# Turning the second attention step's queries and keys on TensorE, and an earlier memset, in a four-layer float32 kernel on one core

## The chip, the core and the metric

One of the eight cores of a Trainium2 chip runs the whole program. Its engines are TensorE (PE in the profile; PEld is its weight load), VectorE (DVE), ScalarE (ACT), GpSimd (POOL) and SyncE (SP, which here only issues DMAs). Each has its own queue, worked off in order, and they wait for each other by semaphores. The metric is the device time of one execution in microseconds (us), lower is better; a time is the median of several runs. One further execution is recorded by the profiler; all rows shown are of that one.

## What is computed

The reference takes `x` of (8, 128, 512), float32, and adds four layers to it one after the other. Cut to what matters here:

```python
x = x + _L0_ffn_ref(_L0_cond_ref(x, ...), ...)
x = x + _L1_ffn_ref(_L1_cond_ref(x, ...), ...)
x = x + _L2_ffn_ref(_L2_cond_ref(x, ...), ...)   # attention, then an expert mix
x = x + _L3_ffn_ref(_L3_cond_ref(x, ...), ...)
```

Layer 2 begins with attention over 32 query heads and 8 key heads of 128 numbers, with a paged cache of 512 keys and values per sequence and 128 new ones:

```python
q = _rope(_rmsnorm(q, q_norm_w), pos)
k = _rope(_rmsnorm(k, k_norm_w), pos)
k_all = jnp.concatenate([kc, k], axis=1)
scores = jnp.einsum('bqhd,bkhd->bhqk', q, k_all) * SCALE
probs = jax.nn.softmax(jnp.where(valid, scores, -1e+30), axis=-1)
o = jnp.einsum('bhqk,bkhd->bqhd', probs, v_all)
```

The result `o` goes through `Wo` and becomes the input of the expert mix.

## The kernel before, in words

The four layers run one after the other, with the work of one beginning among the last work of the layer ahead of it. Layer 2's attention is cut into 32 steps (`steps`): 8 key heads times 4 pairs of sequences. A step `n` handles one key head, its four query heads (`REP`) and two sequences (`j` = 0, 1). Its parts are:

- `project` (products `q_one`, `q_six`, `q_five`, line 971): queries, keys and values of the new tokens, by a scheme of seven block products for eight. It uses PSUM tiles of the tags `mm` (three of them) and `st` (three). The copies and adds that empty them are at lines 1020 and 1025.
- `squares`, `roots`, `rotate`, `rotated`, `normed`: the norm and the rotary turn. GpSimd makes the crossed terms `vq` and `vk` (line 1070). In the first two steps it also makes the inverse root (`roots`, lines 1093 and 1094, by a power). VectorE multiplies by it at line 1104. The result is the tile `r` with ten blocks of 128x128, eight of queries and two of keys.
- Turning: the scores need queries and keys with the head's dimension on the partitions. From step 1 on this takes three moves. `turn(n)` lets VectorE transpose 32x32 blocks into `qkt` (line 1127) and writes it to DRAM in four DMAs (`written`, line 1120). `fetch(n)` reads it back in another order with three DMAs, into `qT` (line 1153) and `kTn` (line 1155); both tiles have one buffer. Step 0 is turned otherwise, by `turn_at_once(0)`: ten transposes on TensorE (line 1145, `turned`) into PSUM, and three copies by ScalarE (line 1147).
- Cached keys and values: `gather(n, "k")` and `gather(n, "v")` issue eight indirect DMAs each from GpSimd's queue (line 914, `kn` and `vals`). `turn_cached` transposes the keys in blocks on VectorE (line 1111, `kt`), and they go through DRAM into `kT` in the same way.
- `weigh(n, j)`: the scores (`st`, line 1165, ten products a sequence) and their exponentials on ScalarE (`pT`, line 1169).
- `mix(n, j)`: products of the weights with the values (`av`, line 1217, ten a sequence), into tiles of the tag `av`, of which there are two.
- `added`, `summed`, `inverted`, `divided`: the sums of the weights, the inverse through DRAM into `R` (line 1210), and the division (`oT`, line 1227).
- `leave(n - 1)`: the output product with `Wo` (`wo_one`, `wo_two`, `wo_six`, line 971), added up in `y2` over the key heads. `y2` is therefore set to zero first, by a memset of 128x4096 numbers on GpSimd (line 1319).

Two functions set the order. `first` makes steps 0 and 1's projections between the last products of layer 1 (`eo_l`, `midp_l`, `midTp_l`, lines 53 and 283, with routing work on VectorE at lines 244 to 272). `run` then goes through the steps; while step `n`'s weights are made, step `n + 1` is projected and turned and step `n - 1` leaves. For `n` = 0 nothing is projected or leaves, since step 1 was projected in `first`.

What is wrapped in `kept` stays in the order in which it is written, on each engine, once `running` holds something; on GpSimd it always does. What isn't wrapped is placed by a scheduler: the memset of `y2` was written at the head of `run`, but it was put behind the gathers of step 1's keys, ahead of step 0's `vq`.

Of the kernel before, what the change touches and what calls it, by code (L numbers as in the profile page):

```python
# [17 lines left out]
P = 128  # L18
NB = 8
# [773 lines left out]
def attention(tc, a, x, ident, lens, kvrow, part, ww, wop, ypool, sums, rot, eps, psa, c2, chunks, mm):  # L793
# [66 lines left out]
    def kept(i):  # L860
        return tc.keep_in_program_order(i) if running or i.ins.engine == pool.engine else i
# [38 lines left out]
    def every(ops):  # L900
        for _ in ops:
            pass
# [186 lines left out]
    def roots(n):  # L1089
        s = S[n]  # L1090
        s["rs"] = rs = wk.tile([P, 2, REP + 1], F32, tag="rs", name=f"rs_{n}")
        if n < 2:
            kept(pool.tensor_scalar(rs, s["ssq"], 1.0 / HD, EPS_RMS, ALU.mult, ALU.add))
            kept(pool.tensor_tensor(rs, rs, half, ALU.pow))
        else:
            kept(act.activation(rs, s["ssq"], AF.Sqrt, bias=eps, scale=1.0 / HD))
# [25 lines left out]
    def turn(n, by=(sp,)):  # L1122

        s = S[n]
        m = 2 * REP
        t = wk.tile([P, 4, m + 2, 32], F32, tag="kt", name=f"qkt_{n}", bufs=1)
        done = kept(dve.transpose(t, s["both"].rearrange("p m (b d) -> p b m d", b=4)))
        s["qT"] = wk.tile([P, 4, m, 32], F32, tag="qT", name=f"qT_{n}", bufs=1)
        s["kn"] = wk.tile([P, 2, 4, 32], F32, tag="kTn", name=f"kTn_{n}", bufs=1)
        written(turned_new[n], t, by)  # L1130
        return done

    def turn_at_once(n):

        s = S[n]
        m = 2 * REP
        s["qT"] = qT = wk.tile([P, 4, m, 32], F32, tag="qT", name=f"qT_{n}", bufs=1)
        s["kn"] = kn = wk.tile([P, 2, 4, 32], F32, tag="kTn", name=f"kTn_{n}", bufs=1)
        for h in (slice(0, REP), slice(REP, m), slice(m, m + 2)):
            k = h.stop - h.start  # L1140
            ps = psa.tile([P, k, P], F32, name=f"turned_{n}_{h.start}", **(
                dict(tag="av") if k == REP else dict(tag="st", bufs=3)
            ))
            for i in range(k):
                kept(pe.transpose(ps[:, i, :], s["both"][:, h.start + i, :], ident))
            to = qT[:, :, h, :].rearrange("p a m t -> p m a t") if k == REP else kn
            kept(act.copy(to, ps.rearrange("p m (a t) -> p m a t", t=32)))

    def fetch(n):
        s = S[n]  # L1150
        m = 2 * REP
        src = turned_new[n].rearrange("b i a m d -> (b i) a m d")
        kept(sp.dma_start(s["qT"], src[:, :, 0:m, :]))
        for j in range(2):
            kept(sp.dma_start(s["kn"][:, j], src[:, :, m + j, :]))
# [32 lines left out]
    def summed(n, j):  # L1188


        s = S[n]
        if j == 0:
            s["rows"] = wk.tile([P, 4, 2, REP * 4], F32, tag="rows", name=f"rows_{n}", bufs=1)
        t = wk.tile([P, REP * 4, 32], F32, tag="part10", name=f"partT_{n}_{j}", bufs=1)
        kept(dve.transpose(t, s["part", j].rearrange("p (b d) -> p b d", d=32)))
        kept(dve.tensor_reduce(s["rows"][:, 0, j, :], t, AX.X, ALU.add))  # L1196
# [91 lines left out]
    def first(mixed, outs_):  # L1288

        every(tokens(0))  # L1290
        running.append(True)
        later = tokens(1, "pT")
        project(0, {
            "u2": lambda: turn_cached(1)(),
            "c22": lambda: every(later),
            "c11": lambda: (squares(0, "k", 0, (0,)), squares(0, "q", 0, (0, 1))),
            "c12": lambda: squares(0, "q", 0, (2, 3)),
        })
        keys_terms = rotate(0)
        mixed()  # L1300

        def rest():
            squares(0, "q", 1, range(REP))
            squares(0, "k", 1, (0,))
            roots(0)
            keys_terms()
            outs_(0)
            outs_(1)
            rotated(0)
            normed(0)  # L1310
            outs_(2, 3)

        project(1, {"one": rest, "c11": lambda: turn_at_once(0)})

    def run(pool_, end_of, bank, keep):
        late.append(pool_)
        y2 = ypool.tile([P, NB, D], F32, tag="y", name="y2")
        Y.append(y2)
        pool.memset(y2, 0.0)

        squares(1, "q", 0, range(REP))
        keys_terms = rotate(1)
        squared(1)
        keys_terms()
        roots(1)
        gather(1, "v")
        rotated(1)
        normed(1)
        turn(1)
        end, prepared = None, iter(())  # L1330
        w_ops, wo_ops = iter(()), WO[0].factors()

        def some(ops, k=1):
            return lambda: [next(ops, None) for _ in range(k)]

        for n, (qd, p) in enumerate(steps):

            after = n + 1 if 0 < n < len(steps) - 1 else None
            weigh(n, 0)
            sums_of, outs = added(n, 0), iter(())  # L1340
            if n == 1:
                some(wo_ops, 2)()
            next(sums_of)
            (some(wo_ops) if n == 1 else some(w_ops))()
            every(sums_of)
            every(w_ops)
            if n:
                divided(n - 1)
                outs = outputs(n - 1)
                if not after:  # L1350
                    every(outs)
            if after:
                project(after, {
                    "u2": lambda: every(outs),
                    "c22": lambda: (turn_cached(2)() if n == 1 else None, some(wo_ops, 3)()),
                    "c11": lambda: (squares(after, "k", 0, (0,)), squares(after, "q", 0, (0, 1))),
                    "c12": lambda: squares(after, "q", 0, (2, 3)),
                })
                keys_terms = rotate(after)
                if n + 2 < len(steps):  # L1360
                    if steps[n + 2][1] == 0:
                        weights(steps[n + 2][0])
                    gather(n + 2, "k")
                leave(n - 1, {
                    "one": lambda: (
                        squares(after, "q", 1, range(REP)), squares(after, "k", 1, (0,)), roots(after),
                    ),
                    "c22": lambda: (every(wo_ops), keys_terms(), rotated(after), normed(after), turn(after)),
                })
                fetch(after)  # L1370
                gather(after, "v")
            mixed = mix(n, 0)
            left = (lambda: leave(n - 1),) if n and not after else ()
            weigh(n, 1, {2: (some(mixed), *left), 3: (some(mixed),), 4: (some(mixed, NC),)})
            sums_of = added(n, 1)
            next(sums_of)
            summed(n, 0)
            if n == 0:
                next(sums_of)
                fetch(1)  # L1380
                gather(2, "k")
            every(sums_of)
            summed(n, 1)
            if 0 < n < len(steps) - 2 and steps[n + 2][1] == 0:
                w_ops = W[steps[n + 2][0]].factors()
            inverted(n, some(w_ops))
            if n + 2 == len(steps):
                end.load_w2()
                end.load_aw()
            if left:  # L1390
                end.shifted()
            if n == 0:
                every(tokens(2))
            if n == 5:
                prepared = end.prepare(bank, lambda shape, name: wk.tile(shape, F32, tag="xs", name=name, bufs=1))
            next(prepared, None)
            every(mix(n, 1))
            next(prepared, None)
            if n and p == 0:
                out_weights(qd)  # L1400
                wo_ops = WO[qd].factors()
            if 0 < n < len(steps) - 2:
                turn_cached(n + 2)()
                some(w_ops)()
                every(tokens(n + 2))
            if n == 3:
                kept(keep())
            if n == 4:
                end = end_of(kept)

            if qd == NQ - 1 and p:
                for j in range(2):
                    end.turn(y2, 2 * (p - 1) + j, bank)
            if n + 2 == len(steps):
                end.low(0, bank)
                end.anchors(0, bank)
        divided(n)
        every(outputs(n))
        end.product(0, "st", bank)
        leave(n)  # L1420
        return y2, end
# [903 lines left out]
```

## Time and profile before

| | us |
|---|---|
| median of 5 runs | 1503.55 |
| lowest and highest | 1501.98 and 1507.11 |
| the profiled execution | 1508.1 |
| its span, from the first to the last instruction | 1506.2 |
| TensorE busy | 1483.0 (98%) |
| VectorE busy | 1070.5 (71%) |
| GpSimd busy | 854.2 (57%) |
| ScalarE busy | 561.3 (37%) |
| mean granted TensorE clock | 0.996 of full speed |

How to read rows of it: in the chain of waits a row is the start, the duration, the engine and the line (`L1165` is line 1165 of the kernel before); the chain is followed back from the last instruction, so what stands in it set the end. In the timeline a row is start, duration, engine, line, operation, output and inputs, the number of instructions run together, and in brackets the idle time ahead of it with what ended it. In the list of waits a row is who waited for whom, the time in total, how often, and the longest. In the tables by stretch a row gives, for PE, PEld, DVE, ACT and POOL, the busy time, and then the granted TensorE clock, the DMA share and GB/s. All times count from the span's start.

### The profile page before, as it was taken

Reading aid. Unit: us, or ns where it says so; the run is one execution under the profiler, and the core shown is the slowest. Engines: PE = TensorE matmul, PEld = TensorE weight load, DVE = VectorE, ACT = ScalarE, POOL = GpSimd, SP = SyncE. Lnnn points to the kernel's source line nnn. Section 1 sums busy time; section 2 is a strip of 40 time slices with the busy share of each in tenths; the row PEclk is TensorE's granted clock in tenths of the full one; section 3 lists DMA queues with packets and bytes.
Section 4 is the critical chain, followed back from the end, with each engine's and each line's share of the span. In section 5 each row is a group of like instructions: output and inputs, shape, how many; then the busy total and the mean of one; then the engine's idle time right before and its main releaser. Section 6 shows DMA issues by size and latency. Waiting matters only on the chain.

```text
span 1506.2 us, 18126 instructions
## 1 busy us (share of the span) xinstructions
PE 1483.0 (98%) x5619; PEld 942.4 (63%) x5619; DVE 1070.5 (71%) x2122; ACT 561.3 (37%) x1419; POOL 854.2 (57%) x874
## 2 busy tenths in 40 slices
PE   8999999999999999999999999999999999999997
PEld 7888787455555565555555555565555555569886
DVE  4566524378788887877778777778877878854475
ACT  1111101044444555444455445455445455431110
POOL 2232103647777677777677777677777777622210
PEclk9999999999999999999999999999999999999999
DMA  7311001204546444454443455445445534432001
GB/s 238 117 43 32 1 1 53 95 29 129 172 136 200 124 145 120 150 175 134 136 153 117 129 155 182 124 134 152 130 128 165 167 105 136 116 123 79 2 15 44
DMA packets 157145, 172.74 MB, mean 115 GB/s; under 512 B 53616, under 2 KB 127536, under 8 KB 156912
## 3 DMA queue, kind: packets, MB, share of 16 engines
q1 hardware_dynamic: 138896, 134.48, 30.2%
q0 software_dynamic: 17056, 36.49, 7.7%
q8 instruction: 47, 0.77, 0.2%
q10 hardware_dynamic: 1088, 0.52, 0.1%
q14 instruction: 58, 0.48, 0.1%
HBM read 130.01 MB, written 41.42 MB: 114 GB/s over the span
## 4 chain that ended last, share of the span: by engine, by line
PE 88%; DVE 5%; DMA 4%; issue 1%; ACT 0%; SPq 0%; ACTq 0%; DVEq 0%
PE st L1165 17%; PE av L1217 15%; PE g L362 8%; PE q_six L971 8%; PE q_one L971 5%; PE q_five L971 5%; PE wo_two L971 5%; PE dn L362 5%; PE wo_one L971 3%; PE wo_six L971 3%; PE eo_l L53 3%; DMA qT<-turned_new 2%; PE h L1753 2%; PE z L1753 2%; PE midp_l L53 1%; PE o L1753 1%
## 5 line engine op out<-in xcount | busy, mean ns | idle before, releaser
L914 POOL DMA_INDIRECT kn<-in_k_cache,kvrow_k x256 | 270.9, 1058 | 76.7 <-issue 66.0
L914 POOL DMA_INDIRECT vals<-in_v_cache,kvrow_v x256 | 270.9, 1058 | 73.5 <-issue 48.2
L1217 PE MATMUL av<-pT,vals 128*128 128x512 f32 x640 | 290.6, 592 | 0.2 <-DVE oT L1227 0.2
L1169 ACT ACTIVATE pT<-st,hide 128x512 f32<-128x512 f32 x256 | 176.0, 687 | 196.4 <-PE st L1165 196.3
L1165 PE MATMUL st<-qT,kT 128*128 128x512 f32 x512 | 238.3, 598 | 4.8 <-DMA qT<-turned_new 4.6
L1217 PEld LDWEIGHTS av<-pT,vals 128*128 128x128 f32 x640 | 121.4, 190 | 153.1 <-issue 145.9
L1070 POOL TENSOR_TENSOR vq<-q,txq 128x256 f32<-128x256 f32 x128 | 121.2, 978 | 144.0 <-ACT sqq L1044 100.8
L1165 PEld LDWEIGHTS st<-qT,kT 128*128 128x128 f32 x512 | 96.6, 191 | 116.6 <-issue 101.7
L1185 DVE TENSOR_TENSOR part<-pT 128x512 f32<-128x512 f32 x128 | 88.4, 692 | 81.3 <-ACT pT L1169 77.0
L971 PE MATMUL q_one<-q,x 128*128 128x384 f32 x256 | 93.0, 486 | 0.0
L1044 ACT ACTIVATE sqq<-q 128x128 f32<-128x128 f32 x252 | 78.2, 310 | 10.7 <-DVE q L1020 4.1
L971 PEld LDWEIGHTS q_one<-q,x 128*128 128x128 f32 x256 | 48.5, 190 | 39.8 <-issue 14.4
L971 PE MATMUL q_six<-q_s,xs_all 128*128 128x384 f32 x192 | 69.8, 486 | 0.0
L1025 ACT COPY q<-q_one 128x256 f32<-128x256 f32 x32 | 11.9, 372 | 148.9 <-PE q_one L971 142.8
L971 PE MATMUL wo_one<-o,oT 128*128 128x256 f32 x256 | 65.8, 379 | 0.4 <-DVE oT L1227 0.4
L1165 PE MATMUL st<-qT,kTn 128*128 128x512 f32 x128 | 65.4, 592 | 0.0
L971 PE MATMUL wo_two<-o_s,os 128*128 128x256 f32 x256 | 60.5, 379 | 0.3 <-DVE os L930 0.3
L429 POOL TENSOR_TENSOR ws<-wu 128x256 f32<-128x256 f32 (+1 forms) x9 | 6.4, 713 | 92.0 <-DMA wu<-in_WuT 81.7
L1169 ACT ACTIVATE pT<-st,rs 128x512 f32<-128x512 f32 x64 | 44.0, 687 | 38.5 <-PE st L1165 38.5
L971 PEld LDWEIGHTS wo_one<-o,oT 128*128 128x128 f32 x256 | 48.6, 190 | 13.9 <-DVE oT L1227 0.6
L1201 ACT COPY rows<-rows 32x32 f32<-32x32 f32 x96 | 20.7, 216 | 97.3 <-DVE rows L1196 96.5
L362 PE MATMUL g<-xs,ws 128*128 128x256 f32 (+1 forms) x240 | 56.1, 384 | 0.0
(459 smaller groups left out, 2850.8 us busy)
## 6 DMA issues: line engine op xcount, KB each, us to landing
turned_new<-qkt SPq DMA_DIRECT2D x124, 160.0 KB
turned_cached<-kt SPq DMA_DIRECT2D x128, 128.0 KB
kT<-turned_cached SPq DMA_DIRECT2D x32, 512.0 KB
R<-sums SPq DMA_DIRECT2D x32, 512.0 KB
qT<-turned_new SPq DMA_DIRECT2D x31, 512.0 KB
q<-in_WqT SPq DMA_DIRECT2D x8, 1024.0 KB
o<-in_WoT SPq DMA_DIRECT2D x8, 1024.0 KB
kn<-in_k_cache,kvrow_k POOLq DMA_INDIRECT x256, 2.8
```

The source lines that it names most:

```text
L53: pe.matmul(o, lhsT, rhs, start=start, stop=stop)
L362: pe.matmul(o, lhsT, rhs, start=start, stop=stop, skip_group_check=True)
L914: kept(pool.indirect_dma_start(out=d[:, c, :], out_offset=None, in_=kc if what == "k" else vc, in_offset=bass.IndirectOffsetOnAxis(ap=kvro ...
L971: kept(pe.matmul(o, l[:, c, :], r[:, c, :], start=start and c == 0, stop=c == 1, skip_group_check=True))
L1044: kept(act.activation(sq, S[n][m][:, j, i, :], AF.Square, accum_out=S[n]["ssq"][:, j, col : col + 1]))
L1070: kept(pool.tensor_tensor(to, t[:, b, :, hi : hi + 64], wx[:, b, lo : lo + 64].unsqueeze(2).to_broadcast(list(to.shape)), ALU.mult,))
L1165: kept(pe.matmul(ps, s["kT"][:, c, 4 * j : 4 * j + 4, :] if c < 4 else s["kn"][:, j], s["qT"][:, :, REP * j : REP * (j + 1), :].rearrange( ...
L1169: kept(act.activation(pT[:, c, :, :].rearrange("p i t -> p (i t)"), ps, AF.Exp, **(dict(bias=hide[:, b, c : c + 1]) if c < 4 else dict(bia ...
L1185: kept(dve.tensor_tensor(o, l, r, ALU.add))
L1201: kept(act.copy(rows[0:32, g, :], rows[32 * g : 32 * g + 32, 0, :]))
L1217: kept(pe.matmul(ps, v[:, c, :], pT[:, c, :, :].rearrange("p i t -> p (i t)"), start=c == 0, stop=c == NC - 1, skip_group_check=True,))
L1753: return pe.matmul(o, lhsT, rhs, start=start, stop=stop, skip_group_check=True)
```

## The change

It has two parts.

The memset of `y2` moves from the head of `run` into `first`, directly behind `roots(0)`, so behind step 0's power on GpSimd. It is wrapped in `kept`: its place on GpSimd is then as written.

Step 1's queries and keys are turned by `turn_at_once(1)` and no longer by `turn(1)` and `fetch(1)`. VectorE's block transpose, four writes and three reads of that step go away; ten TensorE transposes and three ScalarE copies come in. They are written behind the adds of step 0's second sequence, so on TensorE they stand behind the products of step 0's first sequence with the values and ahead of those of the second. Both `av` tiles are in use there, so all three PSUM tiles of step 1's turning are of the tag `st`; step 0 keeps `av` for two of its three. Steps 2 to 31 are turned as before.

```diff
@@ turn_at_once
             ps = psa.tile([P, k, P], F32, name=f"turned_{n}_{h.start}", **(
-                dict(tag="av") if k == REP else dict(tag="st", bufs=3)
+                dict(tag="av") if n == 0 and k == REP else dict(tag="st", bufs=3)
             ))
@@ first, rest
             roots(0)
+            y2 = ypool.tile([P, NB, D], F32, tag="y", name="y2")
+            Y.append(y2)
+            kept(pool.memset(y2, 0.0))
             keys_terms()
@@ run
         late.append(pool_)
-        y2 = ypool.tile([P, NB, D], F32, tag="y", name="y2")
-        Y.append(y2)
-        pool.memset(y2, 0.0)
-
+        y2 = Y[0]
         squares(1, "q", 0, range(REP))
...
         normed(1)
-        turn(1)
         end, prepared = None, iter(())
...
             if n == 0:
                 next(sums_of)
-                fetch(1)
                 gather(2, "k")
             every(sums_of)
+            if n == 0:
+                turn_at_once(1)
             summed(n, 1)
```

## The prediction, made before the change was run

> **What bounds the kernel now.** The page comes first. TensorE (PE) is busy for 1483.0 of 1506.2 us, so what counts is where its stream breaks. The list of what TensorE waited for has two waits of more than 2.1 us:
>
> ```profile
> PE 1483.0 (98%) x5619; PEld 942.4 (63%) x5619; DVE 1070.5 (71%) x2122; ACT 561.3 (37%) x1419; POOL 854.2 (57%) x874
> ...
> PE st L1165 <- DMA qT<-turned_new: 4.6, 5, 2.8
> PE midTp_l L283 <- DVE mw_l L272: 2.9, 1, 2.9
> ```
>
> The second number is the count, the last the longest one. Both are places that the diff touches. The chain of waits around them, and the rows of the timeline, follow.
>
> ```profile
> 292.98 3.76 DVE s_l L268
> ...
> 298.04 0.95 PE midTp_l L283 x4
> 298.99 0.91 PE midp_l L53 x4
> 299.89 4.45 PE eo_l L53 x8
> ...
> 293.17 3.53 POOL L1319 MEMSET y<- 128x4096 f32 x1
> L268 DVE TENSOR_SCALAR s_l<-s_l x6: 160/170/3750, 233.7 to 1438.6; 128x4 f32<-128x4 f32 x6
> L820 DVE TENSOR_SCALAR hide<-hide x1: 1178/1178/1178, 250.7 to 250.7; 128x32 f32<-128x32 f32 x1
> 250.62 2.48 POOL L830 TENSOR_TENSOR txk<-wx_k,sin 128x512 f32<-128x512 f32 x2
> ```
>
> A `tensor_scalar` on four numbers per partition takes 0.17 us (the median of six) and once 3.75. That one ended at 296.73, when the memset of `y2` on GpSimd (POOL) ended, 296.70. The same is seen at 250.7: `hide` ended at 251.88, together with the first of the two POOL products that began at 250.62. So this form of VectorE (DVE) instruction stands still while POOL runs. TensorE paid: its last product before had ended at 295.13 and it went on at 298.04.
>
> ```profile
> 338.35 5.13 PE av L1217 x12
> 343.48 4.46 DMA qT<-turned_new
> 347.93 0.04 issue
> 347.98 6.26 PE st L1165 x10
> ...
> 298.00:299.00 1.00, 0.96 (x5) 0.99 (x6) 0.49 (x1) 0.00 (x0) 0.00 (x0) 0.60 0.00 0
> 300.00:301.00 1.00, 1.00 (x2) 0.48 (x3) 0.00 (x0) 0.37 (x1) 0.00 (x0) 0.50 0.00 0
> 350.00:351.00 1.00, 1.00 (x2) 0.34 (x1) 1.00 (x3) 0.57 (x1) 0.69 (x2) 0.50 0.12 33
> 415.11 4.29 PE st L1165 x10
> ```
>
> Here TensorE ends its `av` products at 345.22 and starts step 1's scores at 347.98, when the turned queries came back from DRAM. In the window rows the third number from the end is the granted clock: 0.50 after either idle time. Step 1's ten score products take 6.26 us, against 4.29 in step 3 (415.11). So each of the two waits costs twice: once itself, once the dip.
>
> **Part 1, the memset leaves 293.17.** Without it, L268 ends at about 293.15; L269, L270 and L272 (0.18, 0.19, 0.69 us and the gaps between) end at 294.3, before TensorE has its last `t` product behind it (eight at 0.43 from 291.43: 294.87). So the transposes start at 294.87, and at full clock take 0.44 (the four at 314.05 do) and not 0.95. The next, `midp_l`, needs `l` (L304, 0.68 us behind the end of `t` at 295.13), so it starts near 295.9 and takes 0.46. The eight `eo_l` take 3.43 (as at 315.78) and end near 299.8. Before, 304.34: 4.5 us. The short hold-up before `midp_l` may cost what one of 0.42 us did at 382.60 (4.56 for 4.29), so I take 4.3. Bounds: 2.91 + 1.98 (0.51 + 0.45 + 1.02 of dip) = 4.9 above; nothing below, if L268 does not meet the memset in most executions. L268 started only 0.19 us before the memset, so a POOL that ran half a microsecond later would let it through. Behind this the stretch to 345 is one TensorE stream with waits of at most 0.2 us, and its other inputs are early: `kn` of step 1 is issued by 293.17 and read at 309.40, and `kT` of step 0 is fetched from 290.20 and used at 327.88. So the gain stays.
>
> **Part 2, the memset arrives behind the power.** On POOL the first power ends at 321.56 and the next work, `vq` of step 1, starts at 327.37 after 5.81 us of idle time that a VectorE result ended. The memset (3.53) fits with 2.28 to spare: POOL's later work, the gathers among it, is not put off. What VectorE does in 321.56 to 325.09 is `r<-r,rs` (L1104), two `x<-eo_l,x` (L300) and two `uq` (L984, L986), all TENSOR_TENSOR. Price: 0 if these ignore POOL, at most 3.53 plus a dip of 1.98 = 5.5 if L1104, which TensorE's `turned` waits for, stands still as L268 did. The nearest row: L1075, `r<-q,tsq` 128x1024, took 1.24 us at 314.65 in the middle of POOL's `vq` products (313.39 to 317.34), and 1.23 and 1.26 at 328.63 and 396.77. I take 0. The Trainium skill (SBUF — State Buffer, Who interferes with whom) says that a VectorE instruction with two SBUF inputs is blocked by a GpSimd one that reads SBUF, not by one that only writes. By it L1075 should have stood still beside `vq`, which the row does not show; for a memset, rule and row both give 0, and the sum is the same by either.
>
> **Part 3, step 1 turned by TensorE.** Removed: VectorE's transpose L1127 (1.51 at 337.32), four writes and three reads on SP's queue (L1120, L1153, L1155; 1.76, 0.61 and 1.29 us of issue), and the wait 2.76 with its dip 1.97. Added, behind step 0's first `av` (six products left from 338.35: 340.93) and ahead of its second: ten transposes, 1.09 us as at 324.37, and three ACT copies, 0.61, 0.61, 0.41. ACT is idle from 339.08 to 347.29, and the bank of each `st` tile is free at 339.08, so the copies are done by 343. The input `r` is ready at 337.29, 3.6 early. The ten `av` left run from 342.0 to 346.3, and step 1's scores follow at once, at full clock, to 350.6 instead of 354.23: 3.64 earlier (2.76 + 1.97 - 1.09). What stood behind the removed issues comes earlier too: VectorE's row sums by 1.5, so `R` is fetched at 349.3 and not 350.83, lands some 3.9 later (the last `R` took 3.92), and `oT` (L1227), its reader, cannot start before 353.5, since the adds ahead of it fill VectorE: no wait.
>
> **Part 4, what is late next.** POOL does not get those 3.64 us. Its 16 gathers follow the second power back to back:
>
> ```profile
> 336.20 2.03 POOL L914 DMA_INDIRECT vals<-in_v_cache,kvrow_v  x1 [0.18 <-issue]
> ...
> 357.48 0.95 POOL L914 DMA_INDIRECT kn<-in_k_cache,kvrow_k  x1 [0.30 <-issue]
> ...
> 360.61 1.29 DVE L1111 STREAM_TRANSPOSE kt<-kn 128x512 f32<-128x512 f32 x2
> 361.83 0.65 DVE L878 TENSOR_TENSOR o_s<-o,o_s 128x512 f32<-128x512 f32 x1
> 362.40 0.41 DVE L1020 TENSOR_TENSOR q<-q_five,uq 128x256 f32<-128x256 f32 x1
> ```
>
> (Part 1 moves all times here alike; I leave it out.) A gather of `kn` lands 2.8 us after its issue (median of the DMA list), so the last, 357.48, lands at 360.3, at the latest by 361.26, when the second `kt` transposed it without a wait. VectorE, 2.6 us earlier by then, wants it at 358.65 and stands for 1.6 to 2.6 us. Behind it in VectorE's queue is `q<-q_five` (L1020), whose PSUM bank the product `wo_two` takes: it becomes free at 362.2 to 363.0 instead of 363.0, while TensorE, 3.6 early, has ended `wo_one` at 360.33. TensorE so stands for 1.9 to 2.7 us and starts `wo_two` 0.8 to 1.7 earlier than before. An idle time of 2.03 us, at 25.12, was followed by a dip: sixteen `g` products took 5.24 from 28.23, and 3.56 from 56.63 (1.7 more). With that the scores of step 2 are reached at 382.2 give or take 0.5, against 382.18; and their own turned queries hang on the same `q`, so they land 0 to 0.85 before 382.56. Net of parts 3 and 4: 0.3 gained of 3.64; between 0.7 lost and, if the gathers land early enough, all 3.64. The skill's page on this (TensorE: Matmul & The Clock Gate, Part 1) wants about 3.4 us without work for a dip; the rows here show one after 2.03, 2.76 and 2.91. By the page TensorE would reach step 2's scores between 380.5 and 381.4 and wait for the fetch, 0 to 0.85 gained, and the whole sum would be near 4.7.
>
> **The sum.** 4.3 + 0 + 0.3 = 4.6 us. The profiled execution took 1508.1 us, 1.9 more than its span, so it becomes 1503.5. It lies 4.55 above the median of the five runs, 1503.55; the same gain there gives 1499.0.
>
> **Rivals.**
> *The gathers land in time*, and part 3 keeps its 3.64: 4.3 + 3.6 = 7.9, 1495.7. For it: no wait is seen at 360.61. Against it: a 2.8 us landing leaves at most 1.0 us of room where 2.6 would be needed.
> *The profiled execution is not the usual one*: it is slower than the median by 4.55 us, nearly the 4.3 of part 1. If L268 slips by the memset in most timed runs, only 0.3 is left: 1503.2. Against it: POOL and VectorE both run down from one product (the end of `t`, 281.7), with little to set them apart, and any memset that starts up to 3.5 us earlier blocks L268 also.
> *The memset stops VectorE at its new place*: L1104 begins at 321.60, 0.04 us behind the power, just as the memset does. If it stands still until 325.09, `turned` comes 2.0 us late, the queue behind it 3.5, and the dip adds 1.98: 5.5 lost against 4.6 won, 1504.5. It decides from 4.6 us on. Against it is the row of L1075.
>
> **How the numbers follow.** Chances: my sum 0.48, gathers in time 0.15, no usual meeting 0.22, memset in the way 0.10, something else 0.05. A difference of 0.2% (3.0 us) is about what a measurement can tell here. Faster by that: most of the first (its gain lies between 3 and 5), the second, a little of the third: 0.60. Within: the rest of the third, half of the fourth and odd ends: 0.28. Slower: half of the fourth, whose price has no row from above, and the unknown: 0.12. The range reaches from the first rival to the third, 1495.5 to 1504.5. My sum's own range is 1497.5 to 1501.
>
> **What would show it.** Part 1: L268 at 0.17 us every time, no wait of `midTp_l`, clock 1.00 through 295 to 300. Part 2: the memset directly behind the power, L1104 at 1.23. Part 3: no wait for `qT` before step 1, scores in 4.29. Part 4: a wait of `kt` for `kn` of 1.6 to 2.6 us, and `wo_two` held by `q`; if `kt` doesn't wait, the first rival is right. I am wrong on the first term if the changed kernel's median is within 2 us of 1503.55 while its profile shows L268 short.

## The result

| | before | after |
|---|---|---|
| median, us | 1503.44 (56 runs) | 1497.06 (29 runs) |
| lowest and highest | 1498.10 and 1509.87 | 1492.78 and 1501.81 |
| profiled execution | 1508.1 | 1497.81 |
| its span | 1506.2 | 1496.0 |

The ratio is 0.9962, 95% interval 0.9953 to 0.9970: the change saves 5.7 us of 1503.44, and the interval reaches from 4.5 to 7.1. The medians lie 6.4 apart, the two profiled executions 10.3.

The page of the changed kernel has TensorE at work for all but 16.1 us of the span; before it was all but 23.2:

```profile
PE 1479.9 (99%) x5629; PEld 942.0 (63%) x5629; DVE 1065.9 (71%) x2121; ACT 562.3 (38%) x1422; POOL 855.6 (57%) x874
```

Its list of what TensorE waited for (total, times, longest) no longer has `midTp_l`, nor any wait of `st` for `qT`. The longest one left, of `gu`, was there before (2.0); the one of `wo_two` is new:

```profile
PE gu L362 <- DVE tgm L369: 2.0, 1, 2.0
PE wo_two L971 <- DVE vals L1020: 1.4, 1, 1.4
```

**Around the old place of the memset.** The rows of L268 in the changed kernel, and then its chain of waits (start, duration, what):

```profile
L268 DVE TENSOR_SCALAR s_l<-s_l x6: 158/170/171, 233.9 to 1430.2; 128x4 f32<-128x4 f32 x6
```

```profile
291.68 3.71 PE t L53 x8
...
295.41 0.70 DVE l L304
...
296.16 0.73 PE midp_l L53 x4
296.89 3.43 PE eo_l L53 x8
```

L268 takes 0.17 us every time, the longest of the six being 171 ns. The eight `eo_l` end at 300.32 and take 3.43, no dip: before, they took 4.45 and ended at 304.34. `t` begins 0.25 later here, so the gain is 4.27 at this point. From the start of `t` to step 0's first scores it was 36.45 us (291.43 to 327.88) and is 32.19 (291.68 to 323.87): 4.26 less.

**Around the memset's new place, and step 1's turning.** The timeline of the changed kernel:

```profile
317.51 3.51 POOL L1308 MEMSET y<- 128x4096 f32 x1
317.58 1.23 DVE L1104 TENSOR_TENSOR r<-r,rs 128x1024 f32<-128x1024 f32 x1 [1.90 <-POOL rs L1094]
318.72 1.28 DVE L300 TENSOR_TENSOR x<-eo_l,x 128x512 f32<-128x512 f32 x2
...
323.36 0.72 POOL L1070 TENSOR_TENSOR vq<-q,txq 128x256 f32<-128x256 f32 x1 [2.34 <-DVE q L1020]
...
336.74 1.25 PE L1145 MATMUL turned<-ident,r 128*128 128x128 f32 x10
...
342.13 3.60 PE L1165 MATMUL st<-qT,kT 128*128 128x512 f32 x8
```

The memset runs right behind the power, and L1104, which begins 0.07 us later, takes its 1.23 us as ever. GpSimd's next work still waits 2.34 us. TensorE turns step 1 at 336.74 and starts its scores at 342.13 with no wait in brackets. From step 0's scores to step 1's it takes 18.26 us, against 20.10, and step 1's ten scores take 4.29 (342.13 to the next product at 346.42) and not 6.26.

**What is late next.** The chain of waits from 353 us on:

```profile
353.36 2.48 DMA kn<-in_k_cache,kvrow_k
...
355.96 0.71 DVE kt L1111
356.68 0.57 DVE o_s L878
357.25 0.34 DVE q L1020
357.58 0.21 DVE vals L1020
...
357.93 1.97 PE wo_two L971 x8
```

The last gather of step 2's keys sets the path: it lands 2.48 us after its issue, VectorE transposes it, frees the PSUM bank by `q` and `vals`, and `wo_two` starts, 1.45 us after TensorE was ready. The table by stretch (PE busy, granted clock, DMA share, GB/s) shows that the clock does not fall behind that stop:

```profile
356.00:358.00 2.00, 0.55 (x4) 1.00 0.20 47
358.00:361.00 3.00, 3.00 (x14) 1.00 0.56 144
```

From step 0's scores to step 2's it was 54.72 us (327.88 to 382.60) and is 52.36 (323.87 to 376.23): 2.36 less. With the 4.26 this makes 6.62 up to step 2, about the difference of the medians. The other 3.6 us between the two spans lie further on. Between step 2's scores and the attention's last ones the changed execution is 2.4 us shorter; of that, 1.45 are three waits of `st` for `qT` (0.22, 0.63 and 0.60) that the recorded execution of before had and this one did not have. Behind TensorE's last product, where the output is written, it is 1.4 shorter. Against both stand the 0.25 us by which `t` began later. Neither place is one that the diff touches, and such waits for `qT` come and go from one execution to the next: the second profile of the change has two again, 2.2 us in all.

### The profile page after: what moved, and what is told of

The parts are those of the page before. It is cut to its first block, busy times and chain, and to the rows that moved or that the text cites. A ratio compares the mean times of both kernels' runs of the same rounds, so it can differ in the third digit from the quotient of the medians.

```text
span 1496.0 us, 18133 instructions
## 1 busy us (share of the span) xinstructions
PE 1479.9 (99%) x5629; PEld 942.0 (63%) x5629; DVE 1065.9 (71%) x2121; ACT 562.3 (38%) x1422; POOL 855.6 (57%) x874
## 4 chain that ended last, share of the span: by engine, by line
PE 92%; DVE 3%; DMA 2%; POOL 1%; issue 1%; ACT 0%; ACTq 0%; DVEq 0%; POOLq 0%
PE st L1165 17%; PE av L1217 17%; PE g L362 9%; PE q_six L971 8%; PE wo_two L971 6%; PE q_one L971 5%; PE q_five L971 5%; PE dn L362 5%; PE wo_six L971 4%; PE wo_one L971 4%; PE eo_l L53 3%; PE h L1753 2%; PE z L1753 2%; PE o L1753 1%; PE midp_l L53 1%; DMA adapter_ids_i<-in_adapter_ids 1%
```

## The experiments

The first theory was the prediction's: each part acts by the wait that it removes, the memset by holding L268, the turning by the queries' way through DRAM; what is gained behind the second is limited by GpSimd's gathers. In all tables "t to st0" is the time from layer 1's second `t` to step 0's first scores, "st0 to st2" that from there to step 2's first scores, both read off the timeline. The ratio is not the quotient of the two medians beside it.

| run | median | before, same chip | ratio, interval | span of its profile | t to st0 | st0 to st2 |
|---|---|---|---|---|---|---|
| before | | | | 1506.2 | 36.45 | 54.72 |
| after | 1497.06 | 1503.44 | 0.9962 [0.9953, 0.9970] | 1496.0 | 32.19 | 52.36 |
| memset only | 1498.39 | 1503.10 | 0.9977 [0.9961, 0.9994] | 1500.3 | 32.39 | 54.50 |
| turning only | 1502.76 | 1503.10 | 1.0001 [0.9980, 1.0023] | 1497.2 | 37.41 | 52.36 |
| after, keys first | 1497.88 | 1503.10 | 0.9968 [0.9952, 0.9983] | 1493.7 | 32.20 | 51.84 |
| before, other form | 1499.36 | 1503.10 | 0.9994 [0.9977, 1.0011] | 1497.3 | 32.34 | 54.38 |
| after again | 1499.76 | 1505.35 | 0.9969 [0.9953, 0.9985] | 1498.4 | 32.37 | 52.48 |
| memset only again | 1501.12 | 1505.35 | 0.9982 [0.9966, 0.9997] | 1502.5 | 32.37 | 53.88 |
| turning only again | 1505.38 | 1505.35 | 1.0004 [0.9984, 1.0024] | 1501.8 | 36.37 | 52.27 |
| after, two memsets | 1501.79 | 1505.35 | 0.9976 [0.9961, 0.9992] | 1507.2 | 32.49 | 53.28 |
| keys first, shifted | 1494.64 | 1504.22 | 0.9936 [0.9916, 0.9957] | 1492.5 | 32.19 | 51.09 |
| after, shifted | 1495.86 | 1501.27 | 0.9968 [0.9954, 0.9981] | 1493.0 | 32.19 | 52.23 |
| keys first, shifted, again | 1494.32 | 1501.27 | 0.9955 [0.9938, 0.9971] | 1494.7 | 32.19 | 50.81 |
| before, shifted | 1501.95 | 1501.27 | 1.0004 [0.9989, 1.0018] | 1503.1 | 37.73 | 52.42 |

### The memset alone

```diff
@@ rest
             roots(0)
+            y2 = ypool.tile([P, NB, D], F32, tag="y", name="y2")
+            Y.append(y2)
+            kept(pool.memset(y2, 0.0))
             keys_terms()
@@ run
-        y2 = ypool.tile([P, NB, D], F32, tag="y", name="y2")
-        Y.append(y2)
-        pool.memset(y2, 0.0)
+        y2 = Y[0]
```

> The memset is moved behind the first power; step 1 is turned through DRAM as before. Theory A (L268 meets the memset in usual executions too): 4 us less than before, 1499.5 where before is 1503.5; the profile shows L268 at 0.17 us, eo_l ending near 300, and the wait of st for qT of step 1 unchanged at 2.8 us with its dip. Theory B (the profiled execution of before was the unusual one): within 1 us of before, though the profile shows L268 short.

The ratio is 0.9977, some 3.5 us, and t to st0 fell by 4.06. A second run gave 0.9982 and 4.08. The line is never longer than 170 ns. In the timeline of the first it even runs in the middle of a gather:

```profile
290.25 0.95 POOL L914 DMA_INDIRECT kn<-in_k_cache,kvrow_k  x1 [0.30 <-issue]
290.48 0.17 DVE L268 TENSOR_SCALAR s_l<-s_l 128x4 f32<-128x4 f32 x1
```

So the gather is not what held it. The gain is there in ordinary executions, and with it falls the rival that the recorded execution was an unusual one: besides, the line is held in all four profiles that have it in its old form and the memset in its old place. Step 1's queries still come late:

```profile
PE st L1165 <- DMA qT<-turned_new: 7.4, 6, 3.1
```

### The turning alone

```diff
@@ turn_at_once
-                dict(tag="av") if k == REP else dict(tag="st", bufs=3)
+                dict(tag="av") if n == 0 and k == REP else dict(tag="st", bufs=3)
@@ run
-        turn(1)
...
-                fetch(1)
                 gather(2, "k")
             every(sums_of)
+            if n == 0:
+                turn_at_once(1)
```

> Step 1 is turned by TensorE; the memset stays where it was. Theory A (the gathers give back part of it, as in the profile of the changed kernel): 2.4 us less than before; the profile shows L268 at 3.7 us, then no wait for qT in step 1, a wait of kt for kn of about 1.5 us and of wo_two for vals of about 1.4. Theory B (my sum): 0.3 less. Theory C (nothing given back): 3.6 less.

The trace has the gain, st0 to st2 52.36 against 54.72, but the times do not: 1.0001, and later 1.0004. The interval of the first, 0.9980 to 1.0023, leaves room for a gain of 3.0 us, so this alone says little; it is taken up below. The memset was in its old place, and the timeline shows it holding the line again, for longer than before:

```profile
288.45 0.94 POOL L914 DMA_INDIRECT kn<-in_k_cache,kvrow_k  x1 [0.30 <-issue]
...
288.68 4.26 DVE L268 TENSOR_SCALAR s_l<-s_l 128x4 f32<-128x4 f32 x1
...
289.39 3.52 POOL L1319 MEMSET y<- 128x4096 f32 x1
```

### Another form of the held instruction

The kernel before with the memset where it was. Only layer 1's L268 becomes a `tensor_tensor` by a tile that holds 1/16.

```diff
+    sixteenth = const.tile([P, 4], F32, tag="sixteenth", name="sixteenth")
+    dve.memset(sixteenth, 1.0 / 16.0)
...
-            dve.tensor_scalar(s, s, 1.0 / mult, None, ALU.mult)
+            if tag == "l1":
+                dve.tensor_tensor(s, s, sixteenth, ALU.mult)
+            else:
+                dve.tensor_scalar(s, s, 1.0 / mult, None, ALU.mult)
```

> The kernel before with the memset left where it was, but layer 1's scaling L268 done by a tensor_tensor with a tile of 1/16 in place of a tensor_scalar. Theory A (only the form of instruction with one tensor input and a constant stands still beside the memset): the instruction takes 0.2 us under the memset, TensorE's wait for mw_l goes, 4 us less than before. Theory B (whatever VectorE starts there stands still until the memset ends): 3.5 us for it or for the reciprocal behind it, and the time of before.

Five lines come in ahead, so L271 here is L268, L277 is L272 and L309 is L304. The timeline:

```profile
290.62 0.16 DVE L271 TENSOR_TENSOR s_l<-s_l,sixteenth 128x4 f32<-128x4 f32 x1
290.82 0.18 DVE L274 RECIPROCAL s_l<-s_l 128x4 f32<-128x4 f32 x1
...
291.26 0.69 DVE L277 TENSOR_TENSOR mw_l<-mid_l,e_l 128x512 f32<-128x512 f32 x1
291.28 3.53 POOL L1324 MEMSET y<- 128x4096 f32 x1
...
292.97 0.69 DVE L309 TENSOR_TENSOR l<-t,mask 128x512 f32<-128x512 f32 x1 [1.01 <-PE t L53]
```

The memset lies in its old place, and beside it VectorE works at its usual 0.69 us (L277 and L309). L271 itself had ended 0.50 us before the memset's row begins. Its counterpart is in the run with the turning alone: there too the line began beside a gather, 0.71 us ahead of the memset (0.66 here), and as a `tensor_scalar` it was held to the memset's end. The product that waited 2.91 us for `mw_l` does not wait, and t to st0 falls by 4.11. So what costs the time is that one form of instruction meets the memset, not that the memset is there; that rests on this profile, on that of the turning alone and on the rows of L1104 above. The median is 3.7 us lower, but the ratio's interval, 0.9977 to 1.0011, holds no change: the trace shows this, the times do not.

### The keys' gathers first

```diff
-        gather(1, "v")
+        gather(2, "k")
...
-                gather(2, "k")
+                gather(1, "v")
```

> The changed kernel with step 2's keys gathered ahead of step 1's values on GpSimd. Theory A (the gathers' landing is what VectorE and then TensorE wait for): the waits of kt for kn and of wo_two for vals between 350 and 358 go away, and 1.3 to 1.6 us with them: 7.8 less than before. Theory B (the next thing, step 2's turned queries through DRAM, is as late): the two waits go, and st waits for qT in step 2 instead: 0 to 0.5 less than the changed kernel. mix of step 1 needs the values only near 366 and should not wait.

`kt` no longer waits for `kn`, nor `wo_two` for `vals`: the gathers' end is what held it. Yet only 0.52 of the 1.45 us came out (st0 to st2 51.84 against 52.36). In its place `wo_one` waited 1.10 us for ScalarE's copy of `k` out of `q_one`, which stands right behind that of `q`:

```profile
354.26 0.37 ACT L1025 COPY q<-q_one 128x256 f32<-128x256 f32 x1 [7.69 <-PE q_six L971]
```

In the changed kernel's profile the same copy followed its product at once (idle 4.68 ahead of it, ended by `q_one`). It comes 3.0 us late here, though no wait of the program asks for `q_six`. The copy was late with the turning alone, too.

### The three again, on one chip

The change, the memset alone and the turning alone once more:

> The whole change, as the yardstick of this call. Theory A (the turning of step 1 on TensorE is worth in an ordinary execution what the traces show, 2.4 us, and the memset move 4.1): 6.5 us under the kernel before, ratio 0.9957, and 2.4 us under the memset-only kernel of this call. Theory B (what step 1 gains is given back by later waits that ordinary executions have and these traces lack): 4.1 us under the kernel before, ratio 0.9973, level with the memset-only kernel within 0.7 us.

> Only the memset moves. Both theories: about 4.1 us under the kernel before, ratio 0.9973, the four-element line at most 0.2 us in the profile, and step 1's scores again held for its queries by 2.8 to 3.2 us. Theory A puts it 2.4 us above the whole change, theory B level with it.

> Only the turning moves; the memset stays behind layer 1's gathers and the four-element line is held 3.5 to 4.3 us. Theory A: 1.3 to 2.4 us under the kernel before, ratio 0.9984 to 0.9991. Theory B: level with before, ratio 0.9996 to 1.0004. The first run of it gave 1.0001 with an interval that holds both. If its copies on ScalarE wait for the later product a second time, wo_one is held 1.1 us again.

The whole change lies 1.4 us under the memset alone (medians 1499.76 and 1501.12), between the 2.4 of theory A and the 0 of B, but the two intervals overlap; the turning alone is again level with before. The traces agree with the first round: st0 to st2 52.48 and 52.27 with the turning, 53.88 without. ScalarE's copy was late again in both kernels with the turning, the whole change among them, which had it on time in its first profile. In the change the lateness cost next to nothing: `wo_one` waited 1.05 and `wo_two` 0.38, together about the 1.45 that `wo_two` had waited alone.

### Two memsets

```diff
             kept(pool.memset(y2, 0.0))
+            kept(pool.memset(y2, 0.0))
```

> The whole change, with the memset of the output issued twice at its new place: 3.5 us more of GpSimd there, against 2.34 us that its next instruction waited. Theory A (the gathers of step 2's keys set wo_two's wait, and a stop of TensorE past about 2 us is followed by about 3 us at half clock): the gathers end 1.2 us later, the wait for kn goes from 1.45 to 2.6 us, wo_two's from 1.4 to about 2.6, a dip follows, and from step 1's scores to step 2's scores it takes 35.3 us without the dip and 37 with it instead of 34.10; time 1.2 to 3 us above the whole change. Theory B (the landing of the gathers is set by the DMA queues, not by their issue): waits as in the whole change, 34.1 us, same time.

The timeline, with GpSimd's idle time ahead of `vq` used up:

```profile
317.79 3.51 POOL L1308 MEMSET y<- 128x4096 f32 x1
321.36 3.51 POOL L1309 MEMSET y<- 128x4096 f32 x1
324.83 4.21 POOL L1070 TENSOR_TENSOR vq<-q,txq 128x256 f32<-128x256 f32 x4
...
354.66 0.95 POOL L914 DMA_INDIRECT kn<-in_k_cache,kvrow_k  x1 [0.30 <-issue]
```

Counted from step 1's scores the last gather is issued 1.02 us later (354.66 less 342.41, against 353.36 less 342.13), and step 1's scores to step 2's take 35.02 instead of 34.10. That is theory A's mechanism, 0.3 below its size; `kt` itself waits for `kn` no longer than in the change (1.47 us), because VectorE too came to it later. The stop came in two pieces, 0.44 ahead of `q_six` and 1.58 ahead of `wo_two`, and no dip followed: the clock stays at 1.00 to 363 us. The time is 2.0 us above the change on the same chip by the medians, in A's range, though the two intervals overlap.

### ScalarE's stream shifted

Eight copies of one element come in on ScalarE between the projections of steps 0 and 1, where it is idle.

```diff
             outs_(1)
+            spare = wk.tile([P, 1], F32, tag="spare", name="spare", bufs=1)
+            for _ in range(8):
+                kept(act.copy(spare, eps))
             rotated(0)
```

First in the kernel with the keys' gathers ahead:

> The keys' gathers first, and eight one-element copies more on ScalarE between the two projections of the beginning, where it waits: every later instruction of ScalarE stands eight places further on in its stream. Theory F (in the kernels with the turning on TensorE, ScalarE's copy of q out of q_one in step 2 comes up to 3 us after its product because of its place in ScalarE's stream, as where its code has to be loaded first): the copy is back within 0.1 us of the end of the q_one product, its idle time before it 4.7 us, wo_one's wait of 1.1 us is gone, and from step 1's scores to step 2's it takes 32.3 to 32.8 us, against 33.58 in the run with the keys first alone; some other instruction of ScalarE is late in its place, where it may cost nothing. Theory P (the copy itself waits for something that the keys-first order or the turning brings): the wait of 7.6 us before the copy, 1.1 us at wo_one and 33.6 us stay. Time: about that of the run with the keys first, at most 1.1 us less.

then in the change, in the first of these once more, and in the kernel before:

> The whole change with the eight one-element copies on ScalarE, the gathers in their old order. Theory F: the copy of q out of q_one comes within 0.1 us of its product, wo_one does not wait; the keys of step 2 still land late, so wo_two waits 1.3 to 1.6 us for its kt, and from step 1's scores to step 2's it takes 34.1 us; time as the change alone, ratio 0.995 to 0.997. Theory G (the eight copies themselves are worth the 3 us by which the last run stood under the change): ratio 0.994 or less. Theory P: the copy waits 7.6 us again.

> The run with the keys first and ScalarE's stream shifted, once more, beside the change shifted alike. Theory F: wo_one and wo_two wait 0.3 us together at most, 32.8 us from step 1's scores to step 2's, and 1.3 us (34.1 less 32.8) under the change shifted alike: ratio to the kernel before 0.994 to 0.996. Theory H (the last run's 0.9936 was a lucky draw of later waits): ratio 0.996 or more, level with the change shifted alike.

> The kernel before with nothing but the eight one-element copies. Theory F: they lie in 4 us of ScalarE's idle time and nothing waits for their place; ratio 1.000 within 0.001, scores of step 1 held for their queries 2.5 to 3.2 us, the four-element line held 3.5 to 4.3. Theory G: 2 to 3 us under the kernel before, ratio 0.998 to 0.9987.

ScalarE's timeline in the keys-first run:

```profile
346.32 0.48 ACT L979 COPY uq<-q_one 128x384 f32<-128x384 f32 x1 [0.54 <-PE q_one L971]
351.48 0.37 ACT L1025 COPY q<-q_one 128x256 f32<-128x256 f32 x1 [4.68 <-issue]
```

The copy is on time in all three kernels with the turning, and step 1's scores to step 2's take 32.83 and 32.55 with the keys first (33.58 unshifted) and 33.97 in the change (34.10). So theory P falls, and G with it: the eight copies alone are worth nothing, in the kernel before (1.0004) or in the change (0.9968). F's first half fits. Its second, that another instruction would be late in the old place, was not seen, so why the copy is late stays open: it was so in five of six profiles of kernels with the turning, in none of the five without it (the shifted one among them), and in none of the three shifted ones with it. It was 2.6 to 3.0 us late.

Keys first and shifted gave 0.9936 and 0.9955, the lowest ratios of all, 1494.64 and 1494.32 us. Beside the change shifted alike it is 1.5 us lower by the medians, as its trace says (1.42 less from st0 to st2); the two intervals overlap, and the whole spans of the two profiles stand the other way round (1494.7 and 1493.0), so the times don't prove that much.

The last of the four brought the surprise. It has the turning through DRAM, and yet st0 to st2 takes 52.42, as with TensorE's turning. The timeline of the kernel before, shifted, and the table by stretch behind the wait:

```profile
349.19 3.70 PE L1165 MATMUL st<-qT,kT 128*128 128x512 f32 x8 [2.75 <-DMA qT<-turned_new]
```

```profile
346.00:349.00 3.00, 0.44 (x2) 1.00 0.91 245
349.00:350.00 1.00, 0.81 (x2) 1.00 0.39 109
350.00:351.00 1.00, 1.00 (x3) 1.00 0.04 8
351.00:352.00 1.00, 1.00 (x4) 1.00 0.24 70
```

The wait is there, 2.75 us as in the profile of before (2.76). The dip is not: the clock stays at 1.00 where it fell to 0.50 there, and the eight scores take 3.70 and not 5.40. Without a dip, in this one execution, the turning on TensorE gains nothing by step 2's scores: 52.42 against 52.23 to 52.48 with it. With a dip (54.72, 54.50, 54.38, 53.88 in the four other profiles with the wait) it gains 2.0 on the mean. That would account for times of the turning between nothing and 2.4 us.

What the two executions differ in is where the stop lies. In each profile the changes of the granted clock lie on one grid of 3.41 us: before, the clock falls at 28.54, 298.20 and 349.40 us, 79 and 15 times 3.413 us apart, each time for 3.41 us. The table by stretch, cut along that grid (PE busy, granted clock, DMA share, GB/s), of before and then of before, shifted:

```profile
342.57:345.98 3.41, 2.64 (x7) 1.00 0.51 131
345.98:349.40 3.42, 1.42 (x4) 1.00 0.70 191
349.40:352.81 3.41, 3.41 (x6) 0.50 0.38 131
...
344.99:348.40 3.41, 1.45 (x4) 1.00 0.67 192
348.40:351.81 3.41, 2.62 (x6) 1.00 0.40 97
```

A stop of the same length had 2.00 us in one stretch, and the clock fell at the end of that stretch; the other had 1.96, and it did not fall. In the three other profiles with this wait, 2.09, 2.18 and 2.37 us of it lay in one stretch, and the clock fell. If a stop of 2.5 to 3.1 us may lie anywhere on the grid, it has the 1.97 or so in one stretch in 58 to 76 of 100 cases. That is an estimate from these lengths; how often ordinary executions have the dip was not measured.

## Why the prediction was right, and where it was wrong

The time, 1497.06, is 1.9 us under the 1499.0 predicted, inside the range given and 0.4 below the likeliest case's own; it is faster by more than 0.2%. The terms:

- **Part 1, 4.3 us for the memset leaving.** Right: 4.26 in the profile, 4.06 to 4.11 in the runs that change only this, some 3.5 and 2.7 by their ratios. The mechanism, L268 held, is shown from both sides: the memset moved, or the form changed in place. Even the 0.35 us hold-up of `midp_l` came as described. Only the upper bound was short: before, shifted, loses 5.5 us here (37.73 against 32.19), since its dip lasted longer and `eo_l` took 5.80 us, not 4.62, and the turning alone loses 5.2, since L268 was held longer. Too wide is the sentence that this form stands still while GpSimd runs: L268 took 0.17 us beside gathers, and four `tensor_scalar` of 128x1 (L812, at 249.40 before) took 0.32 us together beside a GpSimd product.
- **Part 2, nothing for the memset arriving.** Right: L1104 1.23 us, L300 0.64 each, and 2.34 us to spare on GpSimd against 2.28 said. The rival that this memset stops VectorE is out. The three rows of L1075 that the prediction compared all lie beside GpSimd's `vq`; the row without GpSimd is L1104's before, 1.23 us at 321.60 for the same 128x1024, and it bears the reading out.
- **Part 3, 3.64 us at step 1's scores.** Right in the recorded executions: 1.84 for the start and 1.97 for the dip, 3.81. But the dip was counted as certain, and it is not: before, shifted, had the wait without it.
- **Part 4, 3.3 of these given back.** The mechanism is right, the size is the step that failed. The last gather landed after 2.48 us, not 2.8, so `kt` waited 1.45 (1.6 to 2.6 said) and `wo_two` 1.45 (1.9 to 2.7). The dip that I added, 1.7, didn't come. And the queries of step 2 were no limit: from their write's issue to their use it took 9.3 us, where I had carried over 10.4 from before. Net of parts 3 and 4 it became 2.36 in the profile and not 0.3. The first rival, gathers in time, is out all the same: `kt` did wait, and with the gathers put first the wait was gone. That the turning alone was level with before in two runs of ordinary executions, as the 0.3 would have it, is in part luck: 1.7 of what part 4 takes back is a dip that never came.
- **The dip's row.** I took the stop of 2.03 us at 25.12 as the nearest and expected a dip for one of 1.9 to 2.7. The stop was 1.45, and none followed, nor behind 1.58. I went by the length alone and left out where the stop lies on the grid. The Trainium skill (TensorE: Matmul & The Clock Gate, Part 1) wants about 3.4 us without work; thirteen dips behind stops of 1.88 to 3.12 us speak against that length, and the missing one behind 2.75 against any one length that would decide alone.
- **The profiled execution as the measure.** I moved the gain from it to the median unchanged. Between the profiles it was 10.3 us and between the medians 6.4. The stretch up to step 2 gives 6.6; the rest lies in places that the diff does not touch, in later waits for `qT` and in the writing of the output. The 4.6 of the sum lies at the lower edge of the measured 4.5 to 7.1, and 2.0 under what the traces gave up to step 2.

## What to carry to other kernels

A tiny VectorE instruction that sometimes takes the length of a GpSimd instruction is a hold and not work; in the traces it is mended as well by its form (`tensor_tensor` with a constant tile) as by moving the GpSimd instruction. When a wait on the path is removed, look for the engine that didn't gain the time with the rest, since its next result ends the next wait; issue what that wait needs first. And a gain that rests partly on the clock staying up should be given as two numbers, with and without the dip.

## What the runs showed of the hardware

- A `tensor_scalar` of 128x4 stood still for 3.73 to 4.26 us in each of the four profiles in which it met a memset of 128x4096 on GpSimd (3.53 us), and took 0.17 us beside gathers alone. Not every one is held: four of 128x1 took 0.32 us together beside a GpSimd product. In the longest case it began 0.71 us before the memset's row; what held it in that part isn't settled (the gather running then did not hold it elsewhere). A `tensor_tensor` of 128x512 ran beside the memset in 0.69 us, and one of 128x1024 in 1.23. That agrees with the Trainium skill (SBUF — State Buffer, Who interferes with whom) as far as a GpSimd instruction that only writes goes.
- In each of the 14 profiles the changes of the granted clock, up to TensorE's last product, lie on one grid of 3.41 us; it fell to 0.50 for one stretch of it (3.41 us) or, twice, for two (6.83). Behind a stop of TensorE it fell at the end of a stretch of which 1.88 to 2.91 us were idle, 14 times; it did not fall where 1.81 or less were, nor once at 1.96. So the length of the stop alone does not decide: it fell behind stops of 1.88 (memset only again) and 1.89 us (two memsets), and did not behind others of 1.88 (keys first), 1.89 (after again) and 2.75. Two more dips came without such a stop, behind a run of products of 128x16 between the last steps (other form, at 1319.21; two memsets, at 1325.05). What makes the grid isn't shown.
- A copy on ScalarE came about 3 us behind the product it needed, and was on time again when eight tiny copies were put far ahead of it. The cause is open.
